# Field-pair bilinear products on one core: six unsplit pairs instead of fifteen, and field 27 loaded ahead of weight chunk 1

## The chip, the core and the metric

The kernel runs on one core of a Trainium2 chip. The metric is the device time of the program in microseconds (us). Three runs of the kernel before took 750.06, 743.99 and 745.93 us; their median is 745.93 us. Five engines work side by side, each in the order of its own instructions: TensorE (PE, with its weight loads as PEld), VectorE (DVE), ScalarE (ACT), GpSimd (POOL), and SyncE (SP), which only issues transfers. Transfers run on DMA engines that all queues share.

## The reference

The input `x` is 1024 samples by 32 fields by 128 numbers. For each of the 496 pairs of fields (i, j) with i < j there is a 128 by 128 matrix. The result of a pair is x_i times its matrix, multiplied element by element with x_j:

```python
v_i = inputs[:, I_IDX, :]
v_j = inputs[:, J_IDX, :]
transformed = jnp.einsum('bpd,ped->bpe', v_i, W)
return transformed * v_j
```

All of it is 32-bit floating point. The output is 496 x 128 x 1024 numbers, 260 MB; the inputs are 16.8 MB of fields and 32.5 MB of matrices.

## The kernel before

**Tiling.** A field is a tile of 128 partitions by 1024 samples, 512 KB. Pairs are taken by rows: row i holds the pairs (i, i+1) to (i, 31), and rows run from i = 30 down to 0, so that row 30 has one pair and row 0 has 31. Pair q is made in two halves of 512 samples, u = 2q and u = 2q + 1. The loop at the bottom of the function (line 300) runs over u and writes out the order of all engines by hand: `first(u)`, then loads, then `second(u - LAG)` with LAG = 3, then stores, then one task of a list, then differences for DVE.

**Unsplit pairs.** The first `nq0 = NATIVE * (NATIVE + 1) // 2` pairs are unsplit: one 32-bit matmul per half straight from the loaded tiles (line 265), nothing in `second` but the product with x_j on DVE (`write`, line 244). With NATIVE = 5 these are 15 pairs, rows 30 to 26.

**Split pairs.** All others are computed from split operands. `split_w(c)` splits a chunk c of two pairs' matrices: ACT rounds (`wh`, line 149), POOL makes `wl` and `wd` with three operations (lines 151 to 153). `split_x(f, a)` splits half a field: ACT makes `xh` (line 167), POOL makes `xl` with two operations (lines 168 and 169), and DVE later makes `xd` (line 334). A half of a pair is then two matmuls (`xh,wh` and `xl,wl`, line 268), a scaling of the sum in place by ACT (line 270), and in `second` a third matmul onto it (`xd,wd`, line 279). Four sets of split matrices exist (`w_t`, index c modulo 4), and two sets of split fields (`spool`, two buffers). Four PSUM tiles serve the pairs in turn.

**The list of tasks.** `todo` (lines 183 to 192) holds the splits with the pair from which each may be issued and the pair by which it is due, sorted by the latter. At each odd u the first task that may be issued is issued. So at most one split stands behind each pair in the order of ACT and of POOL.

**Loads.** At the start (lines 194 to 202) SP issues weight chunk 0 of eight pairs in two pieces, ACT issues fields 30 and 31, then SP issues fields 29 and 28, weight chunk 1, fields 27 to 24 and weight chunk 2. Later loads follow row by row. Weight tiles have three buffers, so that chunk 3 waits for chunk 0 and so on. `move_on(5)` is a transfer of 640 bytes that POOL issues at u = 2 * nq0.

**Stores.** Results go out in groups of four pairs, 2 MB, and later of three; the first four pairs go singly. ACT issues the stores (line 318), in order with its own work. Twelve pairs' worth of slots and four field groups not yet loaded serve as output buffers.

Of the kernel before, what the change touches and what calls it, by code (L numbers as in the profile page):

```python
# [12 lines left out]
NF = 32  # L13
# [4 lines left out]
WL = 8  # L18
OG = 4
EPS = 2.0**-12  # L20
NATIVE = 5
SHARED = 26
XDLAG = 10
LAG = 3
SPREAD = 18
# [5 lines left out]
XLEAD = 5  # L31
# [26 lines left out]
def kernel(  # L58
# [35 lines left out]
    def load_x(f, pieces=1, eng=None):  # L94
        if f == 0:

            t = rpool.tile([P, WL, P], F32, tag="w", name="x_0").rearrange("p q e -> p (q e)")
        else:
            t = xpool.tile([P, BT], F32, tag=f"x{f}", name=f"x_{f}")
        s = BT // pieces  # L100
        for k in range(pieces):
            (eng or nc.sync).dma_start(out=t[:, k * s : (k + 1) * s], in_=xt[f, :, k * s : (k + 1) * s])
        x_sb[f] = t
# [9 lines left out]
    def load_apart(dst, src):  # L113
        nc.gpsimd.dma_start(out=dst[:ROWS], in_=src[:ROWS].rearrange("(b a) m n -> a b m n", a=NE))
        nc.sync.dma_start(out=dst[ROWS:], in_=src[ROWS:])
# [10 lines left out]
    def load_w(c, splits=(0, WL), eng=nc.sync):  # L126
        w_raw[c] = rpool.tile([P, WL, P], F32, tag="w", name=f"w_{c}")
        if c in WAPART:
            load_apart(w_raw[c], wt[c])
            return  # L130
        for a, b in zip(splits, splits[1:]):
            eng.dma_start(out=w_raw[c][:, a:b, :], in_=wt[c, :, a:b, :])
# [11 lines left out]
    def split_w(c, u):  # L144

        k = c * WC % WL
        raw = w_raw[c * WC // WL][:, k : k + WC, :].rearrange("p q e -> p (q e)")
        h, l, d = w_t[c % 4]
        halved[c] = nc.scalar.mul(h, raw, 1.0 - 2.0**-13)  # L149
        apart(halved[c], halved.get(c - 4), "one engine writes both, in order")  # L150
        nc.gpsimd.tensor_tensor(l, raw, h.bitcast(F32), ALU.subtract)  # L151
        nc.gpsimd.tensor_scalar(d, h.bitcast(F32), EPS, 1.0, ALU.mult, ALU.mult)  # L152
        nc.gpsimd.tensor_tensor(d, l.bitcast(F32), d.bitcast(F32), ALU.subtract)  # L153
        w_s[c] = (h, l, d)
        if (c + 1) * WC % WL == 0:
            spent.append(c * WC // WL)
# [4 lines left out]
    def split_x(f, a, u):  # L161
# [8 lines left out]
        if f == 0 and a > 0:  # L170
            spent.append("x")
        if f > NF - 2 - NATIVE - SHARED:
            later.append((min(u + XDLAG, 2 * first_q[f] + LAG - 1), d, h.bitcast(F32), l.bitcast(F32)))
        else:
            nc.gpsimd.tensor_tensor(d, h.bitcast(F32), l.bitcast(F32), ALU.subtract)

    nq0 = NATIVE * (NATIVE + 1) // 2
    c0 = nq0 // WC
# [5 lines left out]
    for c in range(c0, nchunk):  # L184
        todo.append(((c - 3) * WC + 1, max(c * WC, nq0), lambda u, c=c: split_w(c, u)))
    for i in range(NF - 2 - NATIVE, -1, -1):
        for a in range(0, BT, HB):
            at = first_q[i + 1] + 1 if i < NF - 3 - NATIVE else 2
            if 0 < i < SPREAD:
# [6 lines left out]
    load_x(NF - 1, pieces=2, eng=nc.scalar)  # L196
    load_x(NF - 3)
    load_x(NF - 4)
    load_w(1, eng=nc.sync)
    for f in range(NF - 5, NF - 4 - XLEAD, -1):  # L200
        load_x(f)
    load_w(2, eng=nc.sync)

# [163 lines left out]
```

## Time and profile before

| | |
|---|---|
| runs | 743.99, 745.93, 750.06 us |
| profiled execution, its own time | 741.81 us |
| its span | 739.9 us |
| PE, DVE, ACT, POOL busy | 703.9, 637.3, 634.0, 595.0 us |
| bytes moved | 310.02 MB at 419 GB/s |
| read, written | 49.29 MB, 260.05 MB |

The span runs from the first to the last instruction; the remaining 1.9 us of the execution lie around it. The page lists the groups of instructions by line: the busy time of a group, the mean duration of one, and the idle time of its engine just before it with what ended that. The matmuls of one engine overlap, so that the busy time of PE is not a measure of its load; the distance between the starts of two neighbours is. Of the groups that the change touches:

| line, engine | what | count | mean ns |
|---|---|---|---|
| L265 PE | unsplit matmul, two records a half | 60 | 650 |
| L268, L279 PE | split matmul, three a half | 2886 | 391 to 397 |
| L270 ACT | scaling in PSUM | 962 | 584 |
| L149 ACT | wh | 241 | 410 |
| L167 ACT | xh | 52 | 624 |
| L151, L152, L153 POOL | wl, wd, wd | 241 each | 767, 429, 748 |
| L168, L169 POOL | xl, xl | 52 each | 1292 to 1300, 662 |
| L334 DVE | xd | 52 | 924 |
| L244 DVE | product with x_j, the three groups shown | 485 | 1213 to 1223 |

### The profile page before, as it was taken

The numbers are of one execution on the slowest core, as the hardware profiler recorded it, in microseconds if no ns is written. First come the engines' busy times: TensorE is split into PE (matmuls) and PEld (weight loads), VectorE is DVE, ScalarE is ACT, GpSimd is POOL, SyncE is SP. The second block draws the span as 40 slices with busy tenths as digits, with TensorE's granted clock in tenths as the row PEclk, the third lists the DMA queues.
The fourth block names the chain that finished last, engine by engine and source line by source line (L and its number), as shares of the span: only waits on it lengthen the run. The fifth ranks groups of instructions, "written<-read, shape, count | busy, mean of one in ns | idle before, by whom it ended". The sixth has DMA issues, their size and how long they took to land.

```text
span 739.9 us, 10346 instructions
## 1 busy us (share of the span) xinstructions
PE 703.9 (95%) x2946; PEld 550.4 (74%) x2946; DVE 637.3 (86%) x550; ACT 634.0 (86%) x1256; POOL 595.0 (80%) x882
## 2 busy tenths in 40 slices
PE   7999999999999999999899979999999999999994
PEld 3577777878778888776688758886778887777782
DVE  3898999999999999988798868987999988997884
ACT  1298999999999999998899968998989999898892
POOL 1789999999999999987789776988787888797660
PEclk9999999999999999999999999999999999999997
DMA  9999999999999999999999999999999999999998
GB/s 346 422 429 423 430 413 429 426 418 428 423 421 428 421 426 424 427 418 426 425 427 424 428 425 406 419 424 425 424 425 419 423 421 421 426 416 424 423 430 330
DMA packets 36968, 310.02 MB, mean 419 GB/s; under 512 B 5552, under 2 KB 5680, under 8 KB 19120
## 3 DMA queue, kind: packets, MB, share of 16 engines
q10 hardware_dynamic: 21888, 261.11, 83.6%
q1 hardware_dynamic: 10592, 36.77, 12.4%
q0 software_dynamic: 4432, 11.48, 4.0%
q8 instruction: 24, 0.39, 0.2%
q14 instruction: 32, 0.26, 0.1%
HBM read 49.29 MB, written 260.05 MB: 418 GB/s over the span
## 4 chain that ended last, share of the span: by engine, by line
PE 60%; DMA 22%; DVE 8%; POOL 3%; ACT 3%; issue 2%; ACTq 0%; DVEq 0%; POOLq 0%
PE po L268 38%; DMA out_dram<-slots 20%; PE po L279 18%; DVE slots L244 5%; PE po L265 4%; ACT po L270 2%; DVE xd L334 2%; DMA out_dram<-ot 1%; DVE ot L244 1%; POOL wd L153 1%; POOL wl L151 1%; POOL xl L168 1%; DMA x<-in_xt_dram 1%; POOL xl L169 0%; POOL wd L152 0%
## 5 line engine op out<-in xcount | busy, mean ns | idle before, releaser
L270 ACT ACTIVATE po<-po 128x512 f32<-128x512 f32 x962 | 553.3, 584 | 74.0 <-PE po L268 57.4
L268 PE MATMUL po<-xh,wh 128*128 128x512 f32 x962 | 382.0, 397 | 17.3 <-DVE slots L244 15.2
L279 PE MATMUL po<-xd,wd 128*128 128x512 f32 x962 | 376.4, 391 | 4.8 <-DVE xd L334 2.4
L268 PE MATMUL po<-xl,wl 128*128 128x512 f32 x962 | 377.2, 392 | 1.2 <-POOL wl L151 0.9
L244 DVE TENSOR_TENSOR slots<-po,x 128x1024 f32<-128x1024 f32 (+1 forms) x263 | 314.0, 1213 | 56.3 <-DMA out_dram<-slots 21.1
L268 PEld LDWEIGHTS po<-xh,wh 128*128 128x128 f32 x962 | 181.2, 188 | 74.0 <-DVE slots L244 30.8
L151 POOL TENSOR_TENSOR wl<-w,wh 128x256 fp32r<-128x256 f32 x241 | 184.8, 767 | 63.6 <-ACT wh L149 57.9
L279 PEld LDWEIGHTS po<-xd,wd 128*128 128x128 f32 x962 | 181.2, 188 | 45.0 <-DVE slots L244 3.2
L268 PEld LDWEIGHTS po<-xl,wl 128*128 128x128 f32 x962 | 181.3, 189 | 40.7 <-POOL wl L151 3.9
L153 POOL TENSOR_TENSOR wd<-wl,wd 128x256 fp32r<-128x256 f32 x241 | 180.3, 748 | 20.1
L244 DVE TENSOR_TENSOR slots<-po,x_g 128x1024 f32<-128x1024 f32 x123 | 148.4, 1223 | 22.3 <-DMA out_dram<-slots 8.5
L244 DVE TENSOR_TENSOR ot<-po,x 128x1024 f32<-128x1024 f32 x99 | 119.4, 1221 | 13.6 <-PE po L279 2.6
L152 POOL TENSOR_SCALAR wd<-wh 128x256 fp32r<-128x256 f32 x241 | 103.5, 429 | 20.5
L149 ACT ACTIVATE wh<-w 128x256 fp32r<-128x256 f32 x241 | 98.6, 410 | 5.7 <-DVE slots L244 5.7
L334 DVE TENSOR_TENSOR xd<-xh,xl 128x512 fp32r<-128x512 f32 x52 | 48.0, 924 | 0.0
L168 POOL TENSOR_TENSOR xl<-x_g,xh 128x512 fp32r<-128x512 f32 x32 | 41.6, 1300 | 2.2 <-ACT xh L167 2.0
L168 POOL TENSOR_TENSOR xl<-x,xh 128x512 fp32r<-128x512 f32 x20 | 25.8, 1292 | 15.8 <-ACT xh L167 15.6
L169 POOL TENSOR_SCALAR xl<-xl 128x512 fp32r<-128x512 f32 x52 | 34.4, 662 | 4.6
L265 PE MATMUL po<-x,w 128*128 128x512 f32 x60 | 29.5, 650 | 4.1 <-DMA x<-in_xt_dram 4.1
L265 PEld LDWEIGHTS po<-x,w 128*128 128x128 f32 x60 | 12.1, 207 | 20.7 <-issue 14.5
L167 ACT ACTIVATE xh<-x 128x512 fp32r<-128x512 f32 x20 | 12.3, 624 | 11.5 <-DMA x<-in_xt_dram 11.4
L167 ACT ACTIVATE xh<-x_g 128x512 fp32r<-128x512 f32 x32 | 20.0, 624 | 0.0
(8 smaller groups left out, 49.5 us busy)
## 6 DMA issues: line engine op xcount, KB each, us to landing
out_dram<-slots ACTq DMA_DIRECT2D x67, 1536.0 KB, 12.6
out_dram<-slots ACTq DMA_DIRECT2D x44, 2048.0 KB, 16.5
out_dram<-ot ACTq DMA_DIRECT2D x28, 2048.0 KB, 12.7
w<-in_wt_dram SPq DMA_DIRECT2D x36, 512.0 KB, 10.9
w<-in_wt_dram POOLq DMA_DIRECT2D x25, 448.0 KB, 11.6
x_g<-in_xt_dram SPq DMA_DIRECT2D x16, 512.0 KB, 16.3
x<-in_xt_dram SPq DMA_DIRECT2D x14, 512.0 KB, 9.4
out_dram<-slots ACTq DMA_DIRECT2D x5, 512.0 KB, 8.9
```

Source lines behind the costliest of these rows:

```text
L149: halved[c] = nc.scalar.mul(h, raw, 1.0 - 2.0**-13)
L151: nc.gpsimd.tensor_tensor(l, raw, h.bitcast(F32), ALU.subtract)
L152: nc.gpsimd.tensor_scalar(d, h.bitcast(F32), EPS, 1.0, ALU.mult, ALU.mult)
L153: nc.gpsimd.tensor_tensor(d, l.bitcast(F32), d.bitcast(F32), ALU.subtract)
L168: nc.gpsimd.tensor_tensor(l, x_sb[f][:, s], h.bitcast(F32), ALU.subtract)
L169: nc.gpsimd.tensor_scalar(l, l.bitcast(F32), 1.0 / EPS, 1.0, ALU.mult, ALU.mult)
L244: i = nc.vector.tensor_tensor(ot[:, k, s], p, f, ALU.mult)
L265: nc.tensor.matmul(po[q][:, s], w_raw[q // WL][:, q % WL, :], x_sb[i][:, s], start=True, stop=True)
L268: m = nc.tensor.matmul(po[q][:, s], w_s[c][t][:, r], x_s[i][t][:, s], start=t == 0, stop=t == 1)
L270: scaled[u] = nc.scalar.mul(po[q][:, s], po[q][:, s], 1.0 + EPS)
L279: m = nc.tensor.matmul(po[q][:, s], w_s[q // WC][2][:, r], x_s[i][2][:, s], start=False, stop=True, skip_group_check=True)
L334: nc.vector.tensor_tensor(*later.pop(0)[1:], ALU.subtract)
```

## The change

NATIVE goes from 5 to 3 and SHARED from 26 to 28. With them nq0 goes from 15 to 6: rows 30, 29 and 28 stay unsplit, and rows 27 (pairs 6 to 9) and 26 (pairs 10 to 14) are split like all later ones. SHARED only enters the test `f > NF - 2 - NATIVE - SHARED` (line 172), whose bound is -1 in both, so that DVE makes every `xd` as before. Field 27 is loaded ahead of weight chunk 1.

What follows from nq0 elsewhere: the first split chunk c0 is 3 instead of 7, and four more chunks and four more halves of fields are in the list; fields 27 and 26 are issued from pair 2 on, fields 25 and 24 no longer from pair 2 but from pairs 11 and 16; `move_on(5)` stands at u = 12 instead of u = 30; the load of weight chunk 4 is issued at pair 15 instead of 16.

```diff
-NATIVE = 5
-SHARED = 26
+NATIVE = 3
+SHARED = 28
...
     load_x(NF - 3)
     load_x(NF - 4)
+    load_x(NF - 5)
     load_w(1, eng=nc.sync)
-    for f in range(NF - 5, NF - 4 - XLEAD, -1):
+    for f in range(NF - 6, NF - 4 - XLEAD, -1):
         load_x(f)
     load_w(2, eng=nc.sync)
```

## The prediction

> **What bounds the kernel now.** I read the busy slices first, then a table by stages, then who waits for whom, then POOL's own timeline.
>
> ```profile
> DMA  9999999999999999999999999999999999999998
> GB/s 346 422 429 423 430 413 429 426 418 428 423 421 428 421 426 424 427 418 426 425 427 424 428 425 406 419 424 425 424 425 419 423 421 421 426 416 424 423 430 330
> ```
>
> The transfers are never idle: between the first slice and the last they move 413 to 430 GB/s, one dip (406) apart. 310.02 MB at 424 GB/s are 731 us of a span of 739.9. A change that moves no bytes cannot gain much; it can lose by letting transfers run dry, which nothing makes good later. The stage table (length, engines' busy time, clock, transfer share, GB/s):
>
> ```profile
> 0.00:40.00 40.00, 35.93 (x90) 17.71 (x91) 24.91 (x22) 10.52 (x20) 18.80 (x28) 1.00 0.98 389
> 40.00:80.00 40.00, 37.35 (x160) 29.44 (x159) 36.20 (x33) 36.20 (x74) 36.00 (x50) 1.00 1.01 426
> ...
> 240.00:280.00 40.00, 39.99 (x175) 32.48 (x174) 37.22 (x33) 38.10 (x77) 36.80 (x54) 1.00 1.01 423
> ...
> 320.00:360.00 40.00, 37.97 (x161) 29.37 (x160) 33.19 (x30) 35.20 (x70) 33.11 (x50) 1.00 1.01 422
> ```
>
> POOL (the fifth busy time) has 18.8 us in the first 40, then 36 to 37 in each 40 up to 280, then less. The rest of its time there is the gap between instructions: its waits, by window, are in 0 to 45 us
>
> ```profile
> POOL xl L168 <- ACT xh L167: 15.6, 1, 15.6
> POOL wl L151 <- ACT wh L149: 4.8, 4, 3.4
> ```
>
> and none at all in 45:120, 120:200 and 200:280. From 45 to 280 us POOL runs without a pause and sets the pace of computing. The timeline of POOL shows where its free time lies:
>
> ```profile
> 16.03 1.27 POOL L168 TENSOR_TENSOR xl<-x,xh 128x512 fp32r<-128x512 f32 x1 [15.58 <-ACT xh L167]
> ...
> 31.52 0.75 POOL L111 DMA_DIRECT2D mark<-in_xt_dram x1
> 35.65 0.73 POOL L151 TENSOR_TENSOR wl<-w,wh 128x256 fp32r<-128x256 f32 x1 [3.39 <-ACT wh L149]
> ...
> 45.26 1.30 POOL L168 TENSOR_TENSOR xl<-x,xh 128x512 fp32r<-128x512 f32 x1
> ```
>
> It idles until 16.03 and then 3.39 + 0.47 + 0.46 + 0.52 = 4.84 us up to 43.26. How just in time is it afterwards? Counting L270 operations (one per half pair, in order) dates each half pair on PE. I compared that with POOL's ends: field 23's second half came 0.5 us before its first use (at 51.4 us), field 22's 0.2 (at 64.2), chunks 27 and 32 each 0.2, chunks 50, 60, 65 and 68 each 0.1. So what POOL loses before 45 us, computing loses up to 280 us.
>
> Transfers are sated by a backlog. At 73.88 us, just before a 2 MB store is issued, they had moved 405 GB/s x 73.88 us = 29.9 MB. Issued until then: 12 stores, 18.87 MB, fields 30 to 17, 15 loads with 31, 7.86 MB, chunks 0 to 7, 4.19 MB; together 30.9. The 1.0 MB left last 2.4 us. The same count leaves 4.0 us at 61.08, 4.1 at 67.03, 3.7 at 79.86. Thus **computing may be some 2.4 us late, and every microsecond beyond is lost.** After 280 us DVE waits for stores (29.6 us for slots), so computing is then ahead of transfers again, and a late start no longer matters.
>
> **What the Trainium skill says.** "DMA: Bandwidth & Descriptors", section "Where 436 GB/s comes from", puts the ceiling at 16 ports and 435 GB/s; the best slices here reach 430. Its section "Issuing engines are not separate DMA queues" says that all queues end on the same 16 engines; here three queues' shares add to 100% (83.6, 12.4, 4.0), so the order of loads shifts bytes and makes none. "SBUF — State Buffer", section "Who interferes with whom", says that a VectorE instruction with two SBUF inputs contends with a GpSimd one that reads SBUF. The trace agrees: L169 takes 0.62 us alone and 0.94 to 0.99 at 19 to 25 us, where the four `xd` run; those take 0.68 to 1.32. "Perfetto Trace Analysis", section "GPSIMD Engine Instruction", advises start-to-start spacing for POOL; I price POOL so.
>
> **The change, part by part.**
>
> *PE.* 18 unsplit halves go: two records each, starts 0.43 us apart (11.06, 11.49, 11.92), 15.5 us. 54 split matmuls come at 0.23 us (35.45, 35.67, 35.90), 12.4 us. PE gains 3.1 us, worth nothing while POOL and transfers bind: PE isn't on the path to the end there.
>
> *ACT.* Adds 18 scalings x 0.584 + 4 xh x 0.624 + 4 wh x 0.410 = 14.6 us before about 35 us. ACT was busy 10.5 us of the first 40, so this fits into idle time; its order matters only in holding back POOL, below.
>
> *DVE.* Adds 4 xd x 0.924 = 3.7 us, with DVE busy 24.9 of 40: it fits. They stand behind products in DVE's order, and PE's third matmul of rows 27 and 26 waits for them. I reckon those waits by hand at about 1 us for row 27 and 3 us for row 26 (xd of field 26 at about 28 us). That uses up PE's gain: pair 15 starts near 33.5 us, as before (33.6).
>
> *POOL.* Adds four halves of fields and four chunks. Field 23 with its neighbours (45.26 to 58.11) shows two halves and four chunks in 12.85 us, collisions included; two more halves at 2.09 (45.26 to 47.35) make 17.0 us. Two things pay for it. First the head start: chunk 3 needs only weight chunk 0 (landed at 5.9 us by the trace) and runs in idle time, 2.0 us. Field 27 becomes the fifth transfer on SP; the fifth landed at 11.5 us before, so ACT's xh ends at 12.1 and POOL runs from 12.2 instead of 16.0, 3.8 us. Then the 4.84 us of idle time are filled. The lateness is 17.0 - 2.0 - 3.8 - 4.84 = 6.4 us. If the added work and fields 25 and 24 (9.22 us for four halves, 16.03 to 25.25) meet fewer collisions, at 2.08 and 2.0 us each, it is 4.4. I take 5.5. ACT must stay ahead for this: its xh of field 26 stands behind the scaling of pair 6, near 20 us, and POOL reaches it at 21; it just does.
>
> *move_on(5)* costs POOL 0.75 us in either place; before, it lay ahead of the 3.39 us of idle time, so that it counts in the sum now (it is in what POOL does up to field 22). *Loads on SP:* field 27 lands about 1.3 us earlier (12.7 before), chunk 1 1.3 later (11.5 before). Chunk 1's first use moves from pair 8 unsplit to chunk 4 in ACT's order at 13.1, after 12.7: it just fits. Chunks 3 and 4 wait on buffers that come free a little earlier, chunk 5 on one freed by POOL's chunk 11, near 44 us instead of 39; its first use is pair 40, at 71.5. No bytes come or go. *Early stores:* the first four go 3 us earlier, pairs 4 to 11 about 2 later; the backlog at 30 us (over 1.8 MB of stores and two loads) covers that.
>
> *Sum.* 5.5 us of POOL's lateness, less 0.2 of lead, less 2.4 of backlog at 73.88: **2.9 us**. Later minima, as at 79.86, already carry this loss and ask for no more. The profiled execution's own time is 741.81 (739.9 of span and 1.9 around it), so 744.7; it lies 4.1 below the median of 745.93, on which I predict **749.0**. A measurement of this kernel can tell about 1% from no change, 7.5 us; this is within that.
>
> **Rivals.**
> *A (likeliest, 0.58):* as above. From lateness 4.4 to 6.4 and backlog 2 to 4 us the loss is 0.2 to 4.2.
> *B (0.20), the backlog covers it:* if field 27 lands early, the four halves run without collisions and the load at 73.88 adds more pending bytes than I counted, lateness 4.0 meets 4.0 of backlog. 746, give or take 1.5. For it: 3.7 to 4.1 us at the neighbouring stores; against it: 2.4 at 73.88.
> *C (0.18), slower:* the head start doesn't happen and the idle time isn't filled. POOL's new splits are behind ACT, ACT is behind PE (scaling of pair 6), PE behind DVE's xd, DVE behind POOL: rows of four and five pairs are too short to hide it. With none of the head start, lateness is 17.0 - 4.84 = 12.2, and the loss 12.2 - 2.6 = 9.6: 755.5. It decides from a lateness of 10.1 us on, that is if POOL ends field 22's second half after 74.4 us instead of 64.28. For it: before, ACT waited 5.7 us for DVE in front of wh, and POOL 4.8 for ACT; against it: four ACT operations reach POOL ahead of its queue by my times.
> *D (0.04), faster:* the front is bound by PE after all and its 3.1 us reach the end: 743. Against: transfers are at share 0.98 to 1.01 there.
>
> That the change doesn't do what it says can be excluded but for one thing: all four added xd stay on DVE, since the bound of that test stays at -1.
>
> **Numbers.** A, B and D lie within 1%, C mostly beyond; the three runs before already differ by 6 us, which puts a little of A on either side. Faster by over 1%: 0.02; within: 0.80; slower: 0.18. The range takes in A, half of B below and the lower half of C: 744 to 756.
>
> **What would show it.** A is right if POOL starts xl near 12 us, never waits from there to 280 us, ends field 22's second half near 70 us, and the GB/s of slices 3 to 5 drop by some 3 us' worth. Little or no drop there means B. Idle time on POOL between 12 and 45 us for ACT means C. I am wrong altogether if POOL still has slack at 60 us, or if transfers lose at another place, such as the clock dip at 440 to 480.

## The result and the profile after

The changed kernel took 756.54 us in the median of six runs (751.78 to 761.79), the kernel before 746.61 us in six runs beside it. The ratio is 1.0135, with a 95% interval of 1.0087 to 1.0184. Six further runs gave 753.79 us against 747.68, a ratio of 1.0109 (1.0062 to 1.0156). The change makes the kernel about 1% slower: 8 to 10 us by the ratios (the medians differ by 9.9 and 6.1), with 4.6 to 13.7 us inside the two intervals (0.0062 and 0.0184 of 747). The profiled execution took 755.96 us; its span is 753.7 us, against 739.9 before. The profile before is of an execution some 4 us below its median, so that these 13.8 us are more than the 8 to 10.

First the busy slices of the changed kernel (40 slices of 18.8 us; before, 18.5).

```profile
DMA  9998999999999999999999999999999999999997
GB/s 341 430 417 343 387 406 423 424 426 422 420 418 420 424 424 427 424 427 417 424 428 423 426 426 353 415 426 423 422 424 418 419 420 414 424 414 416 416 392 310
```

Slices 4 to 6 move 343, 387 and 406 GB/s where the kernel before moved 423, 430 and 413. A second hole stands in slice 25 (353; before, 406). The table by stages gives the first one its size (columns as in the prediction: stretch, length, busy time of PE, PEld, DVE, ACT and POOL with counts, clock, transfer share, GB/s).

```profile
0.00:40.00 40.00, 32.12 (x94) 18.14 (x95) 22.99 (x22) 20.71 (x40) 27.33 (x39) 1.00 0.98 386
40.00:80.00 40.00, 34.40 (x145) 26.37 (x144) 34.61 (x31) 32.75 (x66) 36.82 (x51) 1.00 0.94 387
80.00:120.00 40.00, 38.47 (x163) 29.76 (x162) 38.30 (x34) 36.56 (x74) 36.84 (x51) 1.00 0.98 393
120.00:160.00 40.00, 39.87 (x172) 31.75 (x171) 37.65 (x33) 37.85 (x77) 37.01 (x53) 1.00 1.01 426
```

The third of these stages reads, before:

```profile
80.00:120.00 40.00, 38.55 (x164) 30.19 (x163) 37.91 (x33) 36.60 (x74) 36.81 (x53) 1.00 1.01 422
```

Up to 120 us the kernel before had moved (389 + 426 + 422) x 40 = 49.48 MB, this one (386 + 387 + 393) x 40 = 46.64 MB. The 2.84 MB that are missing are 6.7 us at 424 GB/s. The same sum up to 280 us gives 6.9 us, and up to 440 us 7.2: between 120 and 440 us little more is lost. The stretch from 440 to 480 us then moves 390 GB/s against 415, 2.4 us; 2.1 us go between 480 and 720 us, and the rest of the 13.8 us between the spans in the end, where the last transfers run out. The early loss came back in the second profile of the change. The later ones came back in other amounts: by the same sum, 3.0 us between 280 and 440 us and 5.6 between 440 and 480.

Now POOL. Its waits between 0 and 45 us (engine, line and what it waited for; us in total, times, the longest):

```profile
POOL wl L151 <- ACT wh L149: 5.8, 1, 5.8
POOL xl L168 <- ACT xh L167: 4.4, 2, 4.0
```

Between 45 and 280 us it has none. POOL's timeline shows the head start, and where its lateness is read:

```profile
6.26 0.73 POOL L151 TENSOR_TENSOR wl<-w,wh 128x256 fp32r<-128x256 f32 x1 [5.82 <-ACT wh L149]
12.25 1.28 POOL L168 TENSOR_TENSOR xl<-x,xh 128x512 fp32r<-128x512 f32 x1 [3.96 <-ACT xh L167]
...
21.57 1.30 POOL L168 TENSOR_TENSOR xl<-x,xh 128x512 fp32r<-128x512 f32 x1 [0.48 <-ACT xh L167]
...
70.48 0.63 POOL L169 TENSOR_SCALAR xl<-xl 128x512 fp32r<-128x512 f32 x1
71.19 1.06 POOL L151 TENSOR_TENSOR wl<-w,wh 128x256 fp32r<-128x256 f32 x1
```

And the same step, the end of field 22's second half, in the kernel before:

```profile
63.58 0.62 POOL L169 TENSOR_SCALAR xl<-xl 128x512 fp32r<-128x512 f32 x1
64.28 1.06 POOL L151 TENSOR_TENSOR wl<-w,wh 128x256 fp32r<-128x256 f32 x1
```

The chunk that follows starts at 71.19 instead of 64.28: POOL is **6.9 us late**. DVE's timeline shows that the products are late by the same amount. The group that begins with pair 36 starts at 75.44 us here

```profile
75.44 5.32 DVE L245 TENSOR_TENSOR slots<-po,x 128x1024 f32<-128x1024 f32 x4 [0.65 <-PE po L280]
```

and at 68.53 us before:

```profile
68.53 5.32 DVE L244 TENSOR_TENSOR slots<-po,x 128x1024 f32<-128x1024 f32 x4 [0.65 <-PE po L279]
```

So are the stores: three of them are issued at 67.95, 73.95 and 80.79 us instead of 61.08, 67.03 and 73.88. What this does to the transfers is seen in windows of 5 us:

```profile
65.00:70.00 5.00, 5.00 (x24) 4.14 (x23) 4.46 (x5) 4.90 (x11) 4.67 (x7) 1.00 0.63 267
...
80.00:85.00 5.00, 5.00 (x23) 4.13 (x22) 4.73 (x5) 4.87 (x11) 4.66 (x6) 1.00 0.77 324
85.00:90.00 5.00, 4.93 (x20) 3.27 (x19) 5.00 (x6) 4.82 (x11) 4.51 (x8) 1.00 0.98 363
```

Before, these windows moved 415, 421 and 426 GB/s at shares of 0.98 to 1.02. From 65 to 70 us the transfer engines are now idle for a third of the time, while PE is busy throughout. The list of queues for this window (packets, MB, share) has next to nothing but q10, the queue of ACT, which carries the stores; q1, that of SP's loads, has no packet in it:

```profile
q10 hardware_dynamic: 97, 1.33, 62.9%
q14 instruction: 1, 0.01, 0.4%
```

So there were no loads to fill the gap, and the engines waited for the next store. From 85 to 90 us they are almost fully busy and still move only 363 GB/s.

The share column tells the two kinds of loss apart. In the three stages up to 120 us it is 0.98, 1.01 and 1.01 before, and 0.98, 0.94 and 0.98 in the change: the engines were idle for some (0.07 + 0.03) x 40 = 4.0 us more. The other 2.7 of the 6.7 us were lost while they were busy.

### The profile page after: what moved, and what is told of

Its sections match the earlier page's. It is cut to its first block, busy times and chain, and to the rows that moved or that the text cites. A ratio compares the mean times of both kernels' runs of the same rounds, so it can differ in the third digit from the quotient of the medians.

```text
span 753.7 us, 10461 instructions
## 1 busy us (share of the span) xinstructions
PE 705.8 (94%) x2964; PEld 552.2 (73%) x2964; DVE 638.6 (85%) x554; ACT 647.9 (86%) x1282; POOL 612.5 (81%) x902
## 4 chain that ended last, share of the span: by engine, by line
PE 53%; DMA 24%; POOL 8%; DVE 8%; ACT 3%; issue 2%; SPq 0%; ACTq 0%; POOLq 0%; DVEq 0%
PE po L269 35%; DMA out_dram<-slots 21%; PE po L280 17%; DVE slots L245 5%; DMA out_dram<-ot 3%; ACT po L271 2%; POOL xl L168 2%; POOL wd L153 2%; POOL wl L151 2%; DVE xd L335 1%; PE po L266 1%; DVE ot L245 1%; POOL xl L169 1%; POOL wd L152 1%; DMA x<-in_xt_dram 1%
## 5 line engine op out<-in xcount | busy, mean ns | idle before, releaser
L271 ACT ACTIVATE po<-po 128x512 f32<-128x512 f32 x980 | 563.9, 584 | 81.3 <-PE po L269 63.4
L269 PE MATMUL po<-xh,wh 128*128 128x512 f32 x980 | 389.8, 398 | 21.8 <-DVE slots L245 16.7
L280 PE MATMUL po<-xd,wd 128*128 128x512 f32 x980 | 383.8, 392 | 8.8 <-DVE xd L335 2.9
L269 PE MATMUL po<-xl,wl 128*128 128x512 f32 x980 | 384.6, 392 | 4.1 <-POOL xl L169 2.8
L269 PEld LDWEIGHTS po<-xl,wl 128*128 128x128 f32 x980 | 184.6, 188 | 46.3 <-POOL xl L169 5.1
L153 POOL TENSOR_TENSOR wd<-wl,wd 128x256 fp32r<-128x256 f32 x245 | 185.3, 756 | 20.4
L152 POOL TENSOR_SCALAR wd<-wh 128x256 fp32r<-128x256 f32 x245 | 107.0, 437 | 20.9
L168 POOL TENSOR_TENSOR xl<-x,xh 128x512 fp32r<-128x512 f32 x24 | 31.1, 1294 | 4.8 <-ACT xh L167 4.4
L266 PE MATMUL po<-x,w 128*128 128x512 f32 x24 | 15.0, 778 | 4.3 <-DMA x<-in_xt_dram 4.3
L245 DVE TENSOR_TENSOR ot<-po,x_g 128x1024 f32<-128x1024 f32 x13 | 15.9, 1225 | 2.0 <-PE po L280 0.3
## 6 DMA issues: line engine op xcount, KB each, us to landing
w<-in_wt_dram SPq DMA_DIRECT2D x36, 512.0 KB, 10.3
```

The lines of the kernel that those rows point to most:

```text
L168: nc.gpsimd.tensor_tensor(l, x_sb[f][:, s], h.bitcast(F32), ALU.subtract)
L245: i = nc.vector.tensor_tensor(ot[:, k, s], p, f, ALU.mult)
L269: m = nc.tensor.matmul(po[q][:, s], w_s[c][t][:, r], x_s[i][t][:, s], start=t == 0, stop=t == 1)
L271: scaled[u] = nc.scalar.mul(po[q][:, s], po[q][:, s], 1.0 + EPS)
L280: m = nc.tensor.matmul(po[q][:, s], w_s[q // WC][2][:, r], x_s[i][2][:, s], start=False, stop=True, skip_group_check=True)
```

## The experiments

Twelve runs, with two readings for each that can be set against each other: how late the product of pair 36 starts on DVE (against 68.53 us), and how many bytes were missing against the kernel before, in us at 424 GB/s, by the sum shown above, in stages of 40 us. The last column is the measured ratio. The texts on record number their theories anew where they need to; each number holds within its text.

| run | pair 36 late, us | missing by 120 us | by 280 us | ratio (95%) |
|---|---|---|---|---|
| the change | 6.9 | 6.7 | 6.9 | 1.0135 (1.0087 to 1.0184) |
| e1_again | 6.4 | 6.3 | 6.9 | 1.0109 (1.0062 to 1.0156) |
| e2_relief | 10.6 | 10.0 | 10.3 | 1.0174 (1.0133 to 1.0215) |
| e3_pool_late5 | 8.4 | 8.5 | 8.0 | 1.0092 (1.0056 to 1.0129) |
| e4_loads_only | 0.9 | 0.8 | 1.1 | 1.0016 (0.9984 to 1.0048) |
| e5_skip_wd | 2.8 | 2.5 | 2.4 | 1.0087 (1.0055 to 1.0119) |
| e6_pool_late2 | 3.7 | 3.9 | 3.3 | 1.0046 (1.0022 to 1.0069) |
| e7_native4 | 3.3 | 2.8 | 3.3 | 1.0128 (1.0086 to 1.0170) |
| e8_split_only | 10.4 | 10.3 | 10.5 | 1.0136 (1.0093 to 1.0179) |
| e9_before_again | -1.2 | -0.5 | -0.9 | 0.9981 (0.9958 to 1.0005) |
| e11_pool_late2_again | 3.2 | 2.9 | 2.7 | 1.0058 (1.0030 to 1.0086) |
| e12_native6 | 0.0 | 0.0 | -0.1 | 1.0014 (0.9988 to 1.0041) |

Whoever makes the products late by some time has about that time missing from the transfers by 120 us, up to 10.6 us. Two profiles of the same kernel differ too: the second of the kernel before (e9_before_again) is 1.2 us early and has 0.5 us more moved, so that values below about 1 us, e4_loads_only's among them, say little. The ratios follow the early loss only roughly. For e10_native4_again, which repeats e7_native4, only the times are used.

**e1_again: the change once more.** No edit.

> The changed kernel once more, for a second profile and more times. In the first profile it is 13.8 us longer in span: transfers moved 2.8 MB less than before by 120 us (6.5 us at 424 GB/s), the rest went at the clock dip at 440 to 480 us (2.3), between 600 and 720 (2) and in the tail (2). Theory 1 (POOL's lateness alone is what the change costs): the first 120 us lose 6 to 7 us again, and what is lost later varies: 7 to 11 us in the median over before. Theory 2 (the change also costs something in the later stages): the same 2 us each at 600 to 720 and in the tail again, 12 to 14 us in all.

753.79 us. The early loss is the same to within a microsecond. In this profile a later stretch shows what varies from run to run:

```profile
300.00:310.00 10.00, 4.34 (x18) 3.32 (x17) 3.35 (x4) 4.35 (x9) 6.45 (x10) 0.85 1.02 429
310.00:320.00 10.00, 10.00 (x37) 8.06 (x37) 7.76 (x8) 7.46 (x15) 4.49 (x7) 0.81 0.96 401
```

PE has 4.34 us of work in ten, then has all ten filled at a clock of 0.81: it was stalled, and its clock stepped down. The profile of the first run has full clock there.

**e2_relief: POOL relieved of the four new halves.**

```diff
-        nc.gpsimd.tensor_tensor(l, x_sb[f][:, s], h.bitcast(F32), ALU.subtract)
-        nc.gpsimd.tensor_scalar(l, l.bitcast(F32), 1.0 / EPS, 1.0, ALU.mult, ALU.mult)
+        e = nc.vector if f in (26, 27) else nc.gpsimd
+        e.tensor_tensor(l, x_sb[f][:, s], h.bitcast(F32), ALU.subtract)
+        e.tensor_scalar(l, l.bitcast(F32), 1.0 / EPS, 1.0, ALU.mult, ALU.mult)
```

> The changed kernel with the two operations that make xl of fields 27 and 26 on DVE instead of POOL: 8 us off POOL, some 4 on DVE, all else as changed. Theory 1 (POOL's added work): POOL's end of field 22's second half goes from 71.2 back to 63 to 65 us, transfers don't run dry at 60 to 70 us, and the time is that of before within 2 us. Theory 2 (the front of PE, ACT and DVE, or the order of loads, makes the lateness and POOL only follows): no better than the change, 6 us or more over before, since DVE gets more to do.

759.54 us, the slowest of all. POOL did come free; its waits between 10 and 45 us are

```profile
POOL wl L151 <- ACT wh L149: 13.7, 3, 7.0
POOL xl L169 <- ACT xh L167: 2.9, 2, 1.9
```

but pair 36 is 10.6 us late. In the same window PE waits for DVE, which now makes `xl` and `xd`:

```profile
PE po L281 <- DVE xd L336: 7.3, 4, 3.4
```

and its clock falls to 0.66 between 20 and 30 us, which stretches what follows. Taking work from POOL helps only if it doesn't go to another engine of the same chain. The time is what the second theory on record expected, but DVE was given work and the clock fell as well, so that the run doesn't measure POOL's share.

**e3_pool_late5: the kernel before, POOL alone made late,** by five idle repetitions of one operation at field 23.

```diff
-        nc.gpsimd.tensor_tensor(l, x_sb[f][:, s], h.bitcast(F32), ALU.subtract)
+        for _ in range(5 + 1 if (f, a) == (23, 0) else 1):
+            nc.gpsimd.tensor_tensor(l, x_sb[f][:, s], h.bitcast(F32), ALU.subtract)
```

> The kernel before (fifteen unsplit pairs) with five repetitions of the POOL operation that makes xl of field 23's first half, 1.36 us each, 6.8 us, at 45 us, where POOL has no more idle time; nothing else is changed and the result is the same. Theory 1: computing is 6.3 to 6.8 us late from pair 28 on, as in the changed kernel, and transfers lose 4 to 6.5 us by 120 us: 750.5 to 753. Theory 2: POOL alone isn't it: within 2 us of before.

752.74 us, ratio 1.0092. No row is split that wasn't before, no load moved: POOL's lateness by itself slows the kernel by 6.9 us of 747 (4.2 to 9.6). But it is no clean copy of the change: the products are 8.4 us late. The six operations take 8.09 us on POOL, PE stands still meanwhile and comes back at half its clock:

```profile
50.00:55.00 5.00, 0.40 (x2) 0.00 (x0) 1.45 (x2) 1.41 (x4) 4.65 (x5) 0.92 0.97 410
55.00:60.00 5.00, 3.40 (x7) 2.29 (x8) 1.23 (x1) 1.16 (x2) 4.52 (x7) 0.50 0.82 350
60.00:65.00 5.00, 4.89 (x13) 3.34 (x13) 3.25 (x3) 2.37 (x5) 4.02 (x7) 0.56 0.56 214
```

**e4_loads_only: only the order of loads.**

```diff
     load_x(NF - 4)
+    load_x(NF - 5)
     load_w(1, eng=nc.sync)
-    for f in range(NF - 5, NF - 4 - XLEAD, -1):
+    for f in range(NF - 6, NF - 4 - XLEAD, -1):
```

> The kernel before with field 27 loaded ahead of chunk 1 and nothing split more. Both fields and chunk are in place before pair 6 to 8 need them: theory 1 expects no change, within 1.5 us. If the order of loads were what costs, 3 us or more.

749.13 us, ratio 1.0016, no measurable difference. The products are 0.9 us late and 0.8 us are missing by 120 us, no more than two profiles of one kernel differ.

**e6_pool_late2, and again as e11_pool_late2_again:** e3's edit with two repetitions in place of five. They ask whether there is a backlog that covers a short delay.

> The kernel before with two repetitions of the POOL operation at 45 us instead of five, 2.7 us. Theory 1 with a backlog of 2 to 2.4 us: products 2.3 to 2.7 us late at pair 36, but transfers lose at most 0.7 us up to 120 us, no change in time. Theory 3 (there is no usable backlog; what computing is late, transfers lose): transfers lose 2 to 2.7 us by 120 us, and the time is 2 to 3 us over before.

> The kernel before with two POOL operations more at 45 us once more. In its first profile the clock of TensorE was halved for 3.4 us at 54 us, right behind the stall, and products were 3.3 us late instead of 2.5. Theory 1: without such a stretch 2.5 us late, with one 3.3 to 4; by 120 us transfers lose what computing is late less 2 us. Theory 3 (no usable backlog): transfers lose as much as computing is late, and the time is 2 to 5 us over before.

751.42 and 750.94 us, ratios 1.0046 and 1.0058, neither interval reaching 1. Two repetitions are 2.7 us by this kernel's spacing; with the half clock behind the stall they become 3.2 to 3.7 us at pair 36. Nearly all of it is missing: 2.9 us by 120 us in the second run, where the prediction's 2.4 us of backlog would have left 0.8. Its windows show how it is lost:

```profile
80.00:82.50 2.50, 2.50 (x13) 2.05 (x12) 2.50 (x3) 2.44 (x6) 2.33 (x4) 1.00 1.08 419
82.50:85.00 2.50, 2.50 (x11) 1.65 (x10) 2.50 (x4) 2.47 (x6) 2.33 (x4) 1.00 0.81 225
85.00:87.50 2.50, 2.50 (x12) 2.06 (x12) 2.37 (x3) 2.44 (x6) 2.33 (x4) 1.00 1.02 298
```

The engines are idle for a fifth of 2.5 us only, yet 225 and then 298 GB/s are moved. What moves then is loads. From 83.5 to 86.5 us they are alone and fill the engines' time at 238 GB/s:

```profile
DMA packets 191, 0.71 MB, mean 238 GB/s; under 512 B 17, under 2 KB 17, under 8 KB 191
q1 hardware_dynamic: 190, 0.71, 100.1%
```

The engines' idle time by the share column is 1.2 us more than before in this run (0.98, 0.99 and 1.00 in the three stages), 6.0 in e3_pool_late5 (0.98, 0.89, 0.98) and 8.0 in e2_relief (0.97, 0.85, 0.98); each stage is known to 0.2 us. With the change's 4.0 this is the lateness less 2.0 to 2.9 us: pending bytes did keep the engines busy for about the time that was counted. But 1.7 to 2.7 us were lost meanwhile by a lower rate.

**e5_skip_wd: the change with ten chunks cheaper on POOL.** The kernel leaves out the last of the three operations for `wd` in chunks 4 to 13.

```diff
-        nc.gpsimd.tensor_tensor(d, l.bitcast(F32), d.bitcast(F32), ALU.subtract)
+        if not 4 <= c < 14:
+            nc.gpsimd.tensor_tensor(d, l.bitcast(F32), d.bitcast(F32), ALU.subtract)
```

> The changed kernel without POOL's third operation on wd (the subtraction, line 153) for chunks 4 to 13; ten operations at some 0.70 us from start to start, 7.0 us off POOL, no work added anywhere. The wd of pairs 8 to 27 is left as wh times 2^-12, so these pairs are computed with a wrong small term. Theory 1 (POOL's sum sets the lateness): products of pair 36 are 0 to 1.5 us late instead of 6.9, transfers stay full at 60 to 90 us, and the time is within 2 us of before. Theory 2 (the chain PE, ACT, DVE of the short rows sets it, and POOL only runs beside it): still 4 us late or more at pair 36, and 4 us or more over before.

Pair 36 is 2.8 us late instead of 6.9, and by 280 us 2.4 us are missing instead of 6.9. So 4 to 4.5 us of the early loss are POOL's sum of work. Some 2.5 us remained although POOL was relieved by more than the whole lateness (7.5 us, ten times 0.75); it now waited 5.8 and 1.1 us for ACT's `xh` and `wh` between 12 and 60 us, where the change has 4.4. The 2.8 us lie between the two theories on record (0 to 1.5 us, or 4 and more). Between 30 and 80 us PE's longest wait in total is for `xd`:

```profile
PE po L281 <- DVE xd L336: 4.6, 4, 1.9
```

The first transfers go missing between 60 and 100 us:

```profile
40.00:60.00 20.00, 17.66 (x75) 13.63 (x75) 17.53 (x18) 16.97 (x35) 16.95 (x24) 1.00 1.01 425
60.00:80.00 20.00, 18.75 (x82) 14.90 (x81) 18.07 (x17) 18.11 (x38) 18.18 (x24) 1.00 0.98 408
80.00:100.00 20.00, 19.36 (x83) 14.94 (x82) 19.41 (x17) 18.56 (x37) 18.41 (x27) 1.00 0.98 385
```

The time didn't follow: 753.68 us, ratio 1.0087, which is 4.1 to 8.9 us for an early loss of 2.4. Its profile has a stretch at half clock near 301 us that the change's first profile doesn't have. Why the runs of this kernel were not faster is open.

**e7_native4 and e10_native4_again: of the two rows, row 26 alone is split,** loads in the old order; **e8_split_only: rows 27 and 26 split,** loads in the old order.

```diff
-NATIVE = 5
-SHARED = 26
+NATIVE = 4
+SHARED = 27
```

In e8_split_only the two are 3 and 28.

> Half of the change: NATIVE 4, SHARED 27, ten unsplit pairs, only row 26 is split; loads in the order of before. POOL gets two halves and two chunks, 8.4 us, has 4.84 us of idle time and starts 1.3 earlier: theory 1 expects products of pair 36 2 to 3.5 us late and 0 to 3 us over before. Theory 2 (the first short rows in lockstep): row 26 follows unsplit pairs and has five pairs, so less than a third of the loss of the change.

> Ten unsplit pairs once more: it was 3.4 us late at pair 36 in its profile but 7.6 us over before in its median of 6 runs. Theory 1: over more runs it comes out at 3 to 6 us over before. Theory 2: at 7 us or more again.

> The change without the moved load: NATIVE 3, SHARED 28, chunk 1 ahead of field 27. Field 27 lands at 12.7 instead of 11.5 us, and POOL starts on it 1.2 us later. Theory 1: products of pair 36 are 0.7 to 1.3 us later than with the whole change, 7.5 to 8.2 in all, 1 us or so slower than it. Theory 2: no difference.

With row 26 alone pair 36 is 3.3 us late, as expected, and the ratio is 1.0128 in six runs, beyond what was expected, and 1.0064 (1.0034 to 1.0093) in e10 with more runs: slower, by 2.5 to 6.9 us of 747 in the second. With both rows and the old order of loads pair 36 is 10.4 us late (7.5 to 8.2 were expected) and the ratio 1.0136. But 10.2 us at half clock lie in its front (0.73 and 0.76 in the two windows from 20 to 40 us), which can hold PE up by as much as 5.1 us, so the 3.5 us between it and the change are not simply the price of the later load. What the early load saves is thus not measured; that it costs nothing measurable alone is what e4 shows.

**e9_before_again: the kernel before, once more,** to see whether a later loss comes with any profile.

> The kernel before once more, for a second profile. Its first profile (741.8 us) is 5.8 us below the median of 28 runs (747.6), so part of the later lateness of the other kernels against it should be its luck. Theory 1 (the change costs only what is lost by 120 us): the second profile is at 745 to 750 us with the same times up to 280 us, and 3 to 8 us late against the first after that. Theory 2 (the split kernels lose more after 280 us for a reason of their own): no later lateness, within 3 us.

746.59 us, ratio 0.9981. No: this execution has a span of 741.8 us, and nowhere is it more than 1.9 us behind the first profile. On record that was the sign of split kernels losing more later for a reason of their own. It decides little: at 743.6 us this execution, too, is faster than the median.

**e12_native6: one step the other way.** NATIVE 6, SHARED 25.

> The other direction: NATIVE 6, SHARED 25, 21 unsplit pairs, row 25 unsplit as well, loads as before. POOL loses two halves and three chunks, 10 us of work, and has the more idle time; PE makes six more pairs at 1.72 us instead of 1.4. Theory 1: before, transfers are full from 2.5 us on, so there is nothing to gain; 0 to 2 us either way, as long as unsplit pairs and loads keep transfers full up to 45 us; products of pair 36 are between 3 us early and 1 us late. If POOL's lateness were all that counts even there, 3 us or more faster.

747.42 us, ratio 1.0014 (0.9988 to 1.0041): the same as before. POOL has 14.3 us of waits for `wh` in it, up to 120 us, and its products are on time from pair 36 on. No run was faster than the kernel before: a sixth unsplit row gives POOL slack, and the time stays the same.

## Why the prediction was wrong

The direction was right, and the mechanism is in the main the one given. What failed is a term of the sum, and with it the size: 2.9 us were predicted on top of the profiled time, 6.9 were lost early, and the forecast of 749.0 us became 756.5 and 753.8.

**The head start** came as reckoned: POOL took chunk 3 at 6.26 us and field 27 at 12.25 (12.2 predicted). It had no wait from 45 to 280 us.

**The short rows** on PE came as reckoned as well. PE's third matmuls waited 0.16 us in row 27 and 1.55 us in row 26 for `xd`, where 1 and 3 us were set down, and pair 15's second matmul started at 33.94 us (33.61 before; "near 33.5" was predicted). Lateness appeared after it: pair 15's third matmul came at 38.08 us (35.22 before). Before, fields 25 and 24 lay ready by 25 us, so that rows 25 and 24 ran at PE's pace. Now POOL splits them just in time, and pair 24's product was already 5.3 us late.

**POOL's lateness** was mis-sized: I took 5.5 us, halfway down from 6.4 on the hope of fewer collisions; measured were 6.9. The full sum, 17.0 - 2.0 - 3.8 - 4.84 = 6.4, and the wait of 0.48 us at 21.57 make 6.9. The hope wasn't paid out: the four halves of fields 25 and 24 did become cheaper (8.3 us instead of 9.22), but other operations became dearer by as much. Nor do the prices named beside the lower figure of 4.4 give it: four halves and four chunks at 2.08 and 2.0 us are 16.3, four halves at 2.08 are 8.3, which makes 4.8. And "it just does" for `xh` of field 26 was wrong by half a microsecond. By e5, however, the sum is not the whole story: only 4 to 4.5 us went away with the load taken off POOL. Some 2.5 us stayed in that run; which of the waits of PE, ACT and DVE in the front sets this floor wasn't separated.

**The backlog is the step that failed:** "computing may be some 2.4 us late, and every microsecond beyond is lost." e11 lost 2.9 us of 3.2, e7 2.8 of 3.3, the change 6.7 of 6.9. The bytes were counted about rightly: the engines stood idle for the lateness less 2.0 to 2.9 us. But the sum took each pending byte to move at the full rate of 424 GB/s. It didn't: in the change 2.7 us of the 6.7 were lost by a lower rate while the engines were busy. In e11, where this is seen best, loads moved alone, at 238 GB/s. So the term of 2.4 us was worth next to nothing. Why the pending loads were slow wasn't tested. With 5.5 us and no backlog my sum would have given 5.3 us, 751.2; with 6.9 it gives 6.7, 752.6.

**The rivals.** B, a backlog that covers the lateness, is out by the same runs. C has the nearest number (755.5), but not its mechanism: its sign was idle time on POOL for ACT between 12 and 45 us, of which there was 0.48 beyond the expected 3.96, and its point of decision was 74.4 us for the end of field 22's second half, which came at 71.2. Part of its chain is real, however: the 2.5 us that stayed in e5, and PE's waits for `xd` there. D is out: PE's gain reached nothing.

**The rest of the difference.** 6.9 us of 747 are 0.92%, inside both intervals of the change's ratio (1.0087 to 1.0184, 1.0062 to 1.0156). The ratios themselves lie 1 to 3 us above. In the profile of the change another 2.4 us were lost at 440 to 480 us, where a clock dip had been foreseen as a possible place. But the kernel before has that dip too:

```profile
440.00:445.00 5.00, 3.27 (x8) 2.60 (x9) 4.18 (x4) 1.16 (x2) 0.00 (x0) 0.54 1.02 437
```

Behind it that execution lost less, and other runs lose at 300 us or not at all. A rival stays untested here: that kernels with more split rows lose something later for a reason of their own. The two runs with a delay of two repetitions lost in time about what they lost early (3.4 and 4.3 us against 3.3 and 2.7). e5 and e7 lost more (6.5 and 9.6 against 2.4 and 3.3, with the early loss below their intervals), while the repetition of e7 doesn't exclude the early loss alone (2.5 to 6.9). Whether a late start or a split row makes the later losses likelier was not settled.

## What to carry to other kernels

Where transfers bound a kernel, count pending bytes as cover only if a mix that keeps the full rate is pending; here the backlog kept the engines busy, but not at the full rate, and lateness was lost about one for one. The early rows of this kernel are where its slowest helper engine builds its lead: work added there delayed what followed by up to that engine's sum of work, less the idle time that it could truly fill; a hoped-for saving in that sum belongs in the range, not in the forecast. Relieve such an engine only onto one that is not in the same chain.

## What the runs showed of the hardware

**Stalls are paid twice.** After a stop of PE its clock went to half, and the stretches at half clock, the end of each run apart, had three lengths: 3.4, 6.8 and 10.2 us. In e3_pool_late5 a POOL delay at 45 us cost a stretch of 10.2 us from 54 us on; in e8_split_only it was 10.2 us at 25 us, in e2_relief 6.8 us at 21 us. "TensorE: Matmul & The Clock Gate" of the Trainium skill, section "What's actually happening", describes a gate that halves the clock after a window of 4096 cycles, 3413 ns, without enough work, and decides by whole windows. The traces agree: the stretches are one, two and three times 3.41 us. That the stop of another engine, POOL, is enough for it, and that a delay of 2.7 us can come out as 3.7, was not expected.

**Loads without stores beside them were slow.** In the second run with two repetitions they moved 238 GB/s at a share of 1.00 from 83.5 to 86.5 us; in the change 340 GB/s from 87 to 88 us, where loads have 97.7% of the engines' time. The mixed stages move 422 to 426 at 1.01. Why the two differ wasn't tested. A full share is thus no proof of a full rate.
